# Alternating the three pieces of an expert tile with those of its neighbours in a deformable-convolution and mixture-of-experts kernel

## The chip, the cores and the metric

The kernel runs on one core of one Trainium2 chip. The metric is the device time of one execution in microseconds (us), lower is better. Four executions before the change took 6815.22 to 6824.58 us, with a median of 6822.99 us.

## What is computed

The input `x` is four images of 256 channels and 64x64 pixels in float32. First each pixel is normalised over its channels, and three modulated deformable 3x3 convolutions follow, each with a relu; their result is added to `x`. Then every pixel is a token of 256 numbers, which passes a normalisation and a mixture of eight experts, of which the two with the highest gate weights are used for each token:

```python
def _L0_ffn_ref(x, gate_w, gate_b, W1, b1, W2, b2):
    probs = jax.nn.softmax(xf @ gate_w + gate_b, axis=-1)
    top2_vals, top2_idx = jax.lax.top_k(probs, 2)
    ...
        h = jax.nn.gelu(xf @ w1 + bb1, approximate=False)   # 256 -> 512
        y = h @ w2 + bb2                                    # 512 -> 256
        return (acc + we[:, None] * y, None)
...
x = x + _L0_conv_ref(_ln_c(x), ...)
t = _to_tokens(x)
t = t + _L0_ffn_ref(_ln_t(t), ...)
```

## The kernel before

**Convolution.** Twelve stages (a layer of one image each) run one after the other, the images interleaved. A stage has 8 blocks of 512 pixels, and a block 9 taps, so that there are 864 taps. A tap gathers four tiles from a table in memory (`g`, L496, issued by GpSimd as indirect DMAs), interpolates on VectorE (L502, L507) and ScalarE (L510, into `s`), transposes `s` on TensorE (L525, into a PSUM tile `tp`), copies that on ScalarE (L528, `sT`) and multiplies with the tap's weights (L548, `acc`). The PSUM tag `tp` has three buffers, and every transpose of the kernel uses it.

**Experts.** When the last block of an image is done, its tokens are sorted by expert (`route`, `invert`), and 39 tiles of 256 tokens are made of them; the last image is cut into two groups of 23 tiles, so there are 163 tiles in all. The order of a group's tiles takes one from its first half and one from its second in turn, and each half has its own weight buffer, `w[step % 2]`, of 128 x 2308 numbers. Where a tile has the same expert as the one before it in its half, its load is given row numbers beyond the table (`bounds_check`) and moves nothing.

**One tile, in three pieces.** In `expert`, a generator, the first piece adds the bias to the tile before (`products`: `y`, L884 on VectorE, and its store on SP), transposes the tile's tokens `zt` (L832, into a `tp` tile named `ftp`) and copies them to `zT` (L836 on ScalarE, named `fzT` in the profile; one buffer). The second multiplies with W1: two halves of eight matmul records each into `ph` (L848, one PSUM buffer), each followed by two gelu instructions on ScalarE (L858, `hT`, three buffers). The third multiplies with W2, sixteen matmul records into `py` (L866, one PSUM buffer). The load of the next tile's weights (L792) and tokens (L804, two indirect DMAs into two buffers per tag) stands at the head of the third piece, or at the head of the second while the work is being drained.

**When pieces are put in.** `begin` lays the pieces into the lane `tiles`. After every tap `pump` takes as many as their price allows, a third of the group's pace each: paces are 5 taps a tile for the first two groups, 2 for the third, 1.5 for the fourth and 0 for the last. What is left when the taps are over is drained, three pieces at a time (`drain`, and `settle` between some stages). This is the order in which the program names the instructions. The framework then orders each engine's queue by itself: it takes the earliest named instruction that its own cost model thinks ready, so that instructions of a later piece can come before those of an earlier one. `after(x)` only holds an instruction behind `x` on the same engine; it is used for the indirect DMAs (behind the newest gather) and for `y` (behind the newest L507).

Of the kernel before, what the change touches and what calls it, by code (L numbers as in the profile page):

```python
# [8 lines left out]
F32 = mybir.dt.float32  # L9
I32 = mybir.dt.int32  # L10
AF = mybir.ActivationFunctionType
# [3 lines left out]
P = 128  # L15
H = W = 64
C = 256
CC = C // P
# [13 lines left out]
E = 8  # L32
HID = 512
HC = HID // P
FT_LOG = 8
FT = 1 << FT_LOG
FU = FT // P
# [4 lines left out]
W1N = CC * HID + HC  # L42
W2N = HC * C + C
# [29 lines left out]
class Group:  # L73


    def __init__(self, b, n0, n1):
        self.b, self.n0, self.n1 = b, n0, n1
        self.nm = f"{b}_{n0}"
        self.M = (n1 - n0) * TPB

        self.NF = 2 * self.M * P // FT + E - 1


        self.half = (self.NF + 1) // 2
        self.zt, self.acc, self.gy, self.sums, self.py = {}, [], [], [], None
        self.order = [s // 2 + s % 2 * self.half for s in range(self.NF)]


class Lane:
# [5 lines left out]
    def put(self, taps, fn):  # L95
        self.pieces.append((taps, fn))
# [11 lines left out]
class Weave:  # L108
# [672 lines left out]

    def fetch(self, grp, step):

        if self.w is None:
            self.w = [
                self.wt.tile([P, 2, WINN], F32, tag="wt", name=f"w_{i}").rearrange(
                    "p a b -> p (a b)"
                )
                for i in range(2)
            ]  # L790
        f = grp.order[step]
        self.nc.gpsimd.indirect_dma_start(  # L792
            out=self.w[step % 2][:, : W1N + W2N],
            out_offset=None,
            in_=self.ins["W"],
            in_offset=bass.IndirectOffsetOnAxis(ap=grp.wrow[:, f : f + 1], axis=0),
            bounds_check=E * P - 1,
            oob_is_err=False,
        )
        grp.zt[step] = []  # L800
        for u in range(FU):
            zt = self.ffn.tile([P, C], F32, tag=f"zt{u}", name=f"zt_{grp.nm}_{f}_{u}")
            j = FU * f + u
            self.nc.gpsimd.indirect_dma_start(  # L804
                out=zt,
                out_offset=None,
                in_=grp.zd,
                in_offset=bass.IndirectOffsetOnAxis(ap=grp.tok[:, j : j + 1], axis=0),
            )
            grp.zt[step].append(zt)  # L810

    def fetch_next(self, grp, step):
        if step + 1 < grp.NF:
            with self.after(self.gathered):
                self.fetch(grp, step + 1)

    def expert(self, grp, step):

        nc = self.nc
        if step == 0:  # L820
            self.fetch(grp, 0)
            yield
        self.products(grp)
        f = grp.order[step]
        nm = f"{grp.nm}_{f}"
        w = self.w[step % 2]
        w1, w2 = w[:, :W1N], w[:, W1N : W1N + W2N]
        zt = grp.zt.pop(step)
        tp = self.ps.tile([P, CC, FT], F32, tag="tp", name=f"ftp_{nm}")
        for u in range(FU):  # L830
            for c in range(CC):
                nc.tensor.transpose(  # L832
                    tp[:, c, u * P : (u + 1) * P], zt[u][:, c * P : (c + 1) * P], self.ident
                )
        zT = self.ffn.tile([P, CC, FT], F32, tag="zT", bufs=1, name=f"fzT_{nm}")
        nc.scalar.copy(zT, tp)  # L836
        yield

        beside = not self.draining
        if not beside:  # L840
            self.fetch_next(grp, step)
        hT = []
        for h0 in range(0, HC, 2):
            ph = self.ps1.tile([P, 2, FT], F32, tag="ph", name=f"ph_{nm}_{h0}")
            for h in range(2):
                for c in range(CC):
                    o = c * HID + (h0 + h) * P
                    nc.tensor.matmul(  # L848
                        ph[:, h, :],
                        lhsT=w1[:, o : o + P],  # L850
                        rhs=zT[:, c, :],
                        start=(c == 0),
                        stop=(c == CC - 1),
                    )
            ht = self.ffn.tile([P, 2, FT], F32, tag="hT", bufs=3, name=f"hT_{nm}_{h0}")
            for h in range(2):
                k = CC * HID + h0 + h
                nc.scalar.activation(ht[:, h, :], ph[:, h, :], AF.Gelu, bias=w1[:, k : k + 1])  # L858
            hT.append(ht)
        yield  # L860
        if beside:
            self.fetch_next(grp, step)
        py = self.ps1.tile([P, FU, C], F32, tag="py", name=f"py_{nm}")
        for u in range(FU):
            for h in range(HC):
                nc.tensor.matmul(  # L866
                    py[:, u, :],
                    lhsT=hT[h // 2][:, h % 2, u * P : (u + 1) * P],
                    rhs=w2[:, h * C : (h + 1) * C],
                    start=(h == 0),  # L870
                    stop=(h == HC - 1),
                )
        grp.py = (f, py, w2)

    def products(self, grp):

# [81 lines left out]
        put(3, lambda: self.begin(grp))  # L958

    def begin(self, grp):  # L960
        for step in range(grp.NF):
            gen = self.expert(grp, step)
            for _ in range(3 + (step == 0)):
                self.tiles.put(grp.pace / 3, lambda gen=gen: next(gen, None))
        self.tiles.put(grp.pace / 3, lambda: self.products(grp))
        self.tiles.put(3, lambda: self.end(grp))

    def end(self, grp):
# [159 lines left out]
```

## Time and profile before

| what | value |
|---|---|
| median of four executions | 6822.99 us |
| lowest, highest | 6815.22, 6824.58 us |
| the profiled execution, its span | 6832.07 us, 6829.6 us |
| mean granted TensorE clock | 0.979 |
| matmul records of `acc`, `ph`, `py` | 6912, 2608, 2608 |
| busy: TensorE, VectorE, ScalarE, GpSimd | 91%, 72%, 50%, 65% of the span |
| indirect DMAs: gathers, tokens, weights, combine | 3456, 326, 163, 256 |

In the profile PE is TensorE's matmuls, PEld its weight loads, DVE VectorE, ACT ScalarE, POOL GpSimd and SP the queue that issues plain DMAs; a name followed by q is the engine's own queue. `out<-in` names the tile written and the tiles read, "L848" is a line of the kernel. A line of a waits answer is engine, line, what it waited for, microseconds in total, times, longest. A matmul named once in the code is two records here. The recorded length of a matmul holds its passage through the array, so that the records overlap; the distance between starts is what a matmul costs.

### The profile page before, as it was taken

How to read it: one execution, taken by the hardware profiler on the slowest of the kernel's cores; microseconds unless marked ns; L12 is line 12 of the kernel's file. 1: busy time of each engine (PE TensorE's matmuls, PEld its weight loads, DVE VectorE, ACT ScalarE, POOL GpSimd, SP SyncE). 2: the span in 40 equal slices, each digit the busy share in tenths (PEclk: the TensorE clock that was granted, in tenths of full speed). 3: DMA queues.
4: the chain of work that ended last, by engine and by line, in shares of the span. 5: the costliest groups of instructions: out<-in, count | busy, mean ns of one | idle time of the engine just before them, and what ended most of it. 6: DMA issues, size and time to landing. Idle time of an engine off the chain costs nothing. (4 is left out here: it accounts for less than half of the span.)

```text
span 6829.6 us, 88669 instructions
## 1 busy us (share of the span) xinstructions
PE 6225.5 (91%) x26500; PEld 3518.7 (52%) x26500; DVE 4888.6 (72%) x10829; ACT 3437.7 (50%) x7315; POOL 4423.4 (65%) x4245
## 2 busy tenths in 40 slices
PE   7998888888999999999999999999988899988887
PEld 3443344444445555555555455555555566655665
DVE  6777778778999676667878777667778555687511
ACT  4554555555665444446665454445554444554322
POOL 4555766666667666666667777666666766677543
PEclk9999999999999999999999999999999999999998
DMA  8998999999999999999998999989998888899644
GB/s 287 343 347 315 364 346 377 354 353 380 384 395 356 326 349 341 324 337 343 351 356 315 357 359 363 328 334 329 341 341 306 298 286 274 287 359 331 228 136 123
DMA packets 800315, 2223.69 MB, mean 326 GB/s; under 512 B 104728, under 2 KB 302872, under 8 KB 794080
## 3 DMA queue, kind: packets, MB, share of 16 engines
q0 software_dynamic: 551200, 1947.35, 77.1%
q1 hardware_dynamic: 248640, 270.69, 11.6%
q8 instruction: 215, 3.52, 0.2%
q14 instruction: 260, 2.13, 0.1%
HBM read 2160.68 MB, written 196.40 MB: 345 GB/s over the span
## 5 line engine op out<-in xcount | busy, mean ns | idle before, releaser
L496 POOL DMA_INDIRECT g<-tab,idx x3456 | 3624.1, 1049 | 1844.8 <-DVE s L507 736.7
L548 PE MATMUL acc<-sT,wk 128*128 128x512 f32 x6912 | 3389.9, 603 | 164.5 <-ACT sT L528 150.1
L502 DVE SCALAR_TENSOR_TENSOR g<-g,cf 128x512 f32<-128x512 f32 x3456 | 2560.2, 742 | 409.8 <-DMA g<-tab,idx 406.0
L507 DVE SCALAR_TENSOR_TENSOR s<-g,cf 128x256 f32<-128x256 f32 x3456 | 1660.6, 482 | 714.2 <-PE tp L525 427.5
L528 ACT COPY sT<-tp 128x512 f32<-128x512 f32 x1728 | 1001.1, 586 | 1788.1 <-PE tp L525 1782.6
L510 ACT ACTIVATE s<-s,cf 128x256 f32<-128x256 f32 x3456 | 1645.3, 507 | 418.1 <-DVE s L507 409.3
L548 PEld LDWEIGHTS acc<-sT,wk 128*128 128x128 f32 x6912 | 1160.5, 192 | 965.2 <-issue 644.4
L525 PEld LDWEIGHTS tp<-ident,s 128*128 128x128 f32 x6912 | 875.8, 142 | 1393.9 <-issue 652.4
L525 PE MATMUL tp<-ident,s 128*128 128x128 f32 x6912 | 1261.4, 280 | 209.8 <-ACT s L510 189.8
L848 PE MATMUL ph<-fzT,w 128*128 128x256 f32 x2608 | 689.9, 397 | 65.0 <-ACT fzT L836 34.9
L866 PE MATMUL py<-w,hT 128*128 128x256 f32 x2608 | 656.8, 390 | 43.8 <-ACT hT L858 40.0
L848 PEld LDWEIGHTS ph<-fzT,w 128*128 128x128 f32 x2608 | 484.5, 197 | 198.2 <-ACT fzT L836 61.9
L866 PEld LDWEIGHTS py<-w,hT 128*128 128x128 f32 x2608 | 477.5, 192 | 178.9 <-ACT hT L858 83.1
L858 ACT ACTIVATE hT<-ph,w 128x256 f32<-128x256 f32 x652 | 283.4, 471 | 439.1 <-PE ph L848 418.1
L804 POOL DMA_INDIRECT zt<-z,tok x326 | 333.9, 1024 | 163.9 <-issue 88.3
L351 PE MATMUL po<-win,wo 128*32 128x504 f32 (+1 forms) x2304 | 356.0, 594 | 5.0 <-ACT win L295 3.2
L792 POOL DMA_INDIRECT w<-in_W,wrow x163 | 177.5, 1089 | 269.7 <-issue 104.9
L907 POOL DMA_INDIRECT gy<-ys,slots x256 | 264.1, 1031 | 109.6 <-issue 65.7
L884 DVE TENSOR_TENSOR y<-py,w 128x512 f32<-128x512 f32 x163 | 111.4, 684 | 228.8 <-PE py L866 228.8
L922 DVE SCALAR_TENSOR_TENSOR ta<-gy,cw,ta 128x256 f32<-128x256 f32 x256 | 120.5, 479 | 132.3 <-DMA gy<-ys,slots 77.2
L351 PE MATMUL po<-win_pre,wo 128*32 128x504 f32 (+1 forms) x1152 | 187.0, 610 | 3.4 <-ACT om L360 3.1
L351 PEld LDWEIGHTS po<-win,wo 128*32 128x32 f32 x2304 | 72.8, 109 | 174.4 <-issue 140.5
(152 smaller groups left out, 2980.9 us busy)
## 6 DMA issues: line engine op xcount, KB each, us to landing
tab<-hv SPq DMA_DIRECT2D x512, 128.0 KB
g<-tab,idx POOLq DMA_INDIRECT x3456
ys<-y SPq DMA_DIRECT2D x163, 256.0 KB
tab<-h_pre SPq DMA_DIRECT2D x128, 256.0 KB
wk<-in_conv_w SPq DMA_DIRECT2D x99, 256.0 KB
xc_pre<-in_x SPq DMA_DIRECT2D x32, 512.0 KB
xr_tok<-in_x SPq DMA_DIRECT2D x32, 512.0 KB
t<-t_tok SPq DMA_DIRECT2D x32, 512.0 KB
```

The source lines that it names most:

```text
L351: nc.tensor.matmul(po[g * Q : (g + 1) * Q, :].rearrange("q (r w) -> q r w", w=W)[:, :, x0:x1], lhsT=self.wo[l][:, 3 * ky + kx, c, :], rhs= ...
L496: self.gathered = nc.gpsimd.indirect_dma_start(out=g.rearrange("p x s f -> p (x s f)"), out_offset=None, in_=self.table(*self.stages[i]), ...
L502: nc.vector.scalar_tensor_tensor(g[:, :, 0, :], g[:, :, 1, :], cf[:, j, 0:1], g[:, :, 0, :], ALU.mult, ALU.add,)
L507: self.last = nc.vector.scalar_tensor_tensor(s, g[:, 1, 0, :], cf[:, j, 1:2], g[:, 0, 0, :], ALU.mult, ALU.add)
L510: nc.scalar.activation(s, s, AF.Copy, scale=cf[:, j, 2:3])
L525: self.turned = nc.tensor.transpose(tp[:, c, u * P : (u + 1) * P], ss[u][:, c * P : (c + 1) * P], self.ident)
L528: nc.scalar.copy(self.sT[:, :, t0 * P : (t0 + 2) * P], tp)
L548: nc.tensor.matmul(acc[:, o, :], lhsT=self.wk[k][:, c, o * P : (o + 1) * P], rhs=sT[:, c, :], start=(k == 0 and c == 0), stop=(k == K - 1 ...
L804: self.nc.gpsimd.indirect_dma_start(out=zt, out_offset=None, in_=grp.zd, in_offset=bass.IndirectOffsetOnAxis(ap=grp.tok[:, j : j + 1], axi ...
L848: nc.tensor.matmul(ph[:, h, :], lhsT=w1[:, o : o + P], rhs=zT[:, c, :], start=(c == 0), stop=(c == CC - 1),)
L858: nc.scalar.activation(ht[:, h, :], ph[:, h, :], AF.Gelu, bias=w1[:, k : k + 1])
L866: nc.tensor.matmul(py[:, u, :], lhsT=hT[h // 2][:, h % 2, u * P : (u + 1) * P], rhs=w2[:, h * C : (h + 1) * C], start=(h == 0), stop=(h == ...
```

## The change

The generator `expert` becomes three functions: `tile_turn` (transposes and the copy to `zT`), `tile_hidden` (`products` of the tile before, W1 and gelu) and `tile_out` (W2, then the loads). `begin` lays them in another order: W2 of tile s-1, W1 of tile s, transposes of tile s+1. The loads are split: `tile_out` of tile s issues the weights of tile s+1 and the tokens of tile s+2; while draining, `tile_hidden` of tile s issues the weights of s+1. `have` keeps a load from being issued twice. A group has one piece more. The buffers of all tiles stay as they were.

```diff
-        self.zt, self.acc, self.gy, self.sums, self.py = {}, [], [], [], None
+        self.zt, self.acc, self.gy, self.sums, self.py = [], [], [], [], None
+        self.have = 0
 ...
     def fetch(self, grp, step):
+        if step >= grp.NF:
+            return
+        f = grp.order[step]
+        for u in range(FU):
+            zt = self.ffn.tile([P, C], F32, tag=f"zt{u}", name=f"zt_{grp.nm}_{f}_{u}")
+            j = FU * f + u
+            with self.after(self.gathered):
+                self.nc.gpsimd.indirect_dma_start(out=zt, ...)
+            grp.zt.append(zt)
+
+    def weights(self, grp, step):
+        if step < grp.have or step >= grp.NF:
+            return
+        grp.have = step + 1
 ...
+        with self.after(self.gathered):
             self.nc.gpsimd.indirect_dma_start(
+                out=self.w[step % 2][:, : W1N + W2N],
 ...
+    def tile_turn(self, grp, step):
+        ...
+        tp = self.ps.tile([P, CC, FT], F32, tag="tp", name=f"ftp_{nm}")
+        for u in range(FU):
+            zt = grp.zt.pop(0)
+            ...
+        grp.zT = self.ffn.tile([P, CC, FT], F32, tag="zT", bufs=1, name=f"fzT_{nm}")
+        nc.scalar.copy(grp.zT, tp)
+
+    def tile_hidden(self, grp, step):
+        self.products(grp)
+        if self.draining:
+            self.weights(grp, step + 1)
+        ...  (W1 and gelu as before)
+
+    def tile_out(self, grp, step):
+        if step >= 0:
+            ...  (W2 as before)
+            grp.py = (grp.order[step], py, w2)
+        self.weights(grp, step + 1)
+        self.fetch(grp, step + 2)
 ...
     def begin(self, grp):
+        put, part = self.tiles.put, grp.pace / 3
+        put(part, lambda: (self.weights(grp, 0), self.fetch(grp, 0)))
+        put(part, lambda: self.tile_turn(grp, 0))
         for step in range(grp.NF):
-            gen = self.expert(grp, step)
-            for _ in range(3 + (step == 0)):
-                self.tiles.put(grp.pace / 3, lambda gen=gen: next(gen, None))
-        self.tiles.put(grp.pace / 3, lambda: self.products(grp))
+            put(part, lambda step=step: self.tile_out(grp, step - 1))
+            put(part, lambda step=step: self.tile_hidden(grp, step))
+            put(part, lambda step=step: self.tile_turn(grp, step + 1))
+        put(part, lambda: self.tile_out(grp, grp.NF - 1))
+        put(part, lambda: self.products(grp))
         self.tiles.put(3, lambda: self.end(grp))
```

More of the change, by code (lines that the diff above doesn't have):

```diff
@@ L782, in fetch @@
     def fetch(self, grp, step):
+        if step >= grp.NF:
[5 more added lines that the diff above has]
+            with self.after(self.gathered):
+                self.nc.gpsimd.indirect_dma_start(
+                    out=zt,
+                    out_offset=None,
+                    in_=grp.zd,
+                    in_offset=bass.IndirectOffsetOnAxis(ap=grp.tok[:, j : j + 1], axis=0),
+                )
+            grp.zt.append(zt)
[3 more added lines that the diff above has]
+        grp.have = step + 1
         if self.w is None:
@@ L791, in fetch @@
         f = grp.order[step]
[L792 to L803, printed above, removed]
+        with self.after(self.gathered):
@@ L804, in fetch @@
             self.nc.gpsimd.indirect_dma_start(
-                out=zt,
+                out=self.w[step % 2][:, : W1N + W2N],
                 out_offset=None,
-                in_=grp.zd,
-                in_offset=bass.IndirectOffsetOnAxis(ap=grp.tok[:, j : j + 1], axis=0),
-            )
[L810 to L817, printed above, removed]
-        nc = self.nc
[L820 to L828, printed above, removed]
+                in_=self.ins["W"],
@@ L829, in expert @@
+                in_offset=bass.IndirectOffsetOnAxis(ap=grp.wrow[:, f : f + 1], axis=0),
+                bounds_check=E * P - 1,
+                oob_is_err=False,
+            )
+    def tile_turn(self, grp, step):
+        if step >= grp.NF:
+            return
+        nc = self.nc
+        nm = f"{grp.nm}_{step}"
         tp = self.ps.tile([P, CC, FT], F32, tag="tp", name=f"ftp_{nm}")
         for u in range(FU):
+            zt = grp.zt.pop(0)
             for c in range(CC):
                 nc.tensor.transpose(
-                    tp[:, c, u * P : (u + 1) * P], zt[u][:, c * P : (c + 1) * P], self.ident
+                    tp[:, c, u * P : (u + 1) * P], zt[:, c * P : (c + 1) * P], self.ident
@@ L834, in expert @@
                 )
[L835 to L842, printed above, removed]
+        grp.zT = self.ffn.tile([P, CC, FT], F32, tag="zT", bufs=1, name=f"fzT_{nm}")
+        nc.scalar.copy(grp.zT, tp)
+    def tile_hidden(self, grp, step):
+        nc = self.nc
+        self.products(grp)
+        if self.draining:
+            self.weights(grp, step + 1)
+        w = self.w[step % 2]
+        grp.hT = []
@@ L843, in expert @@
         for h0 in range(0, HC, 2):
-            ph = self.ps1.tile([P, 2, FT], F32, tag="ph", name=f"ph_{nm}_{h0}")
+            nm = f"{grp.nm}_{step}_{h0}"
+            ph = self.ps1.tile([P, 2, FT], F32, tag="ph", name=f"ph_{nm}")
             for h in range(2):
@@ L849, in expert @@
                         ph[:, h, :],
-                        lhsT=w1[:, o : o + P],
-                        rhs=zT[:, c, :],
+                        lhsT=w[:, o : o + P],
+                        rhs=grp.zT[:, c, :],
                         start=(c == 0),
@@ L854, in expert @@
                     )
-            ht = self.ffn.tile([P, 2, FT], F32, tag="hT", bufs=3, name=f"hT_{nm}_{h0}")
+            ht = self.ffn.tile([P, 2, FT], F32, tag="hT", bufs=3, name=f"hT_{nm}")
             for h in range(2):
                 k = CC * HID + h0 + h
[L858 to L873, printed above, removed]
+                nc.scalar.activation(ht[:, h, :], ph[:, h, :], AF.Gelu, bias=w[:, k : k + 1])
+            grp.hT.append(ht)
+    def tile_out(self, grp, step):
+        if step >= 0:
+            w2 = self.w[step % 2][:, W1N : W1N + W2N]
+            py = self.ps1.tile([P, FU, C], F32, tag="py", name=f"py_{grp.nm}_{step}")
+            for u in range(FU):
+                for h in range(HC):
+                    self.nc.tensor.matmul(
+                        py[:, u, :],
+                        lhsT=grp.hT[h // 2][:, h % 2, u * P : (u + 1) * P],
+                        rhs=w2[:, h * C : (h + 1) * C],
+                        start=(h == 0),
+                        stop=(h == HC - 1),
+                    )
+            grp.py = (grp.order[step], py, w2)
+        self.weights(grp, step + 1)
+        self.fetch(grp, step + 2)
     def products(self, grp):
```

## The prediction

> **What bounds the kernel now.** I read the page first: its head, its busy line and its slices.
>
> ```profile
> span 6829.6 us, 88669 instructions
> PE 6225.5 (91%) x26500; PEld 3518.7 (52%) x26500; DVE 4888.6 (72%) x10829; ACT 3437.7 (50%) x7315; POOL 4423.4 (65%) x4245
> PE   7998888888999999999999999999988899988887
> DMA  8998999999999999999998999989998888899644
> ```
>
> From slice 13 on, where expert tiles run beside taps, TensorE and the DMA engines are both at eight or nine tenths; only in the last three slices does the DMA fall off. The kernel is shared between two limits until about 6330 us and is a chain of expert tiles after that. I therefore split the waits there. First the stretch with both (2160 to 6330 us), in the view of waits; the last two numbers of a line are how often and the longest.
>
> ```profile
> PE tp L525 <- ACT s L510: 115.3, 132, 2.8
> PE acc L548 <- ACT sT L528: 40.6, 68, 1.6
> PE ph L848 <- ACT fzT L836: 34.9, 51, 1.3
> PE py L866 <- ACT hT L858: 24.1, 48, 1.4
> PE ph L848 <- ACT hT L858: 4.8, 7, 1.8
> PE tp L525 <- ACT sT L528: 4.1, 4, 1.4
> ...
> DVE g L502 <- DMA g<-tab,idx: 373.1, 249, 10.8
> DVE s L507 <- PE tp L525: 303.4, 308, 4.7
> ```
>
> Within the tiles' three steps TensorE waits 34.9 + 24.1 + 4.8 = 63.8 us here; these are what the change can touch. The last two lines say who is behind whom in the taps: VectorE waited 303 us for TensorE to free `s`, and 373 us for gathers to land. So TensorE is the limit in about 303 / (303 + 373) = 45% of it.
>
> Then one tile of that stretch in the timeline (start, duration, engine; in brackets the idle time before and who ended it):
>
> ```profile
> 4326.15 0.60 PE L832 MATMUL ftp<-ident,zt 128*128 128x128 f32 x4
> 4327.43 0.70 PE L848 MATMUL ph<-fzT,w 128*128 128x256 f32 x2 [0.67 <-ACT fzT L836]
> ...
> 4334.38 0.70 PE L866 MATMUL py<-w,hT 128*128 128x256 f32 x2 [0.35 <-ACT hT L858]
> ```
>
> The transposes and the W1 products are named a whole piece apart (5/3 taps), yet run next to each other: the framework pulls a piece forward once its inputs should be there. So the waits come from adjacency in that order, not in the program's. Last, the drain:
>
> ```profile
> 6727.59 1.89 PE L848 MATMUL ph<-fzT,w 128*128 128x256 f32 x8
> ...
> 6729.31 0.60 PE L832 MATMUL ftp<-ident,zt 128*128 128x128 f32 x4
> ...
> 6730.58 1.89 PE L848 MATMUL ph<-fzT,w 128*128 128x256 f32 x8
> ...
> 6733.09 2.86 PE L866 MATMUL py<-w,hT 128*128 128x256 f32 x12 [0.19 <-ACT hT L858]
> ```
>
> Between the two halves of W1 stand the transposes of a later tile: the framework has already moved them ahead of this tile's W2. W2 begins every 8.20 us here (6733.09, 6741.29, 6749.49). TensorE's waits from 6330 to 6780 us:
>
> ```profile
> PE ph L848 <- DMA w<-in_W,wrow: 24.5, 9, 8.6
> PE py L866 <- ACT hT L858: 15.9, 21, 8.0
> ```
>
> **The change part by part.**
>
> *Transposes moved ahead of W2.* Per tile they issue four records at L832, no DMA, and one copy (0.586 us). In the stretch before 6330 us, `ph` of tile s+1 now finds `zT` filled, since sixteen W2 records (3.45 us in the chain of waits) and the copy lie between. That removes the 51 waits, 34.9 us. Bounds: 0 if the framework still sets them side by side, 34.9 if all go. I take 34.9. What is late next there is `w`, taken up below.
>
> *Transposes as filler.* The tokens of tile s+2 are asked for a tile earlier, so the four transposes (0.6 us a set) can stand in a gelu wait. 55 waits cost 24.1 + 4.8 = 28.9 us, 0.53 us each; a set fits one of a tile's two gaps, and some are filled by taps already. Bounds 0 to 28.9; I take 12, somewhat under half.
>
> *The drain.* About 40 tiles (644 `ph` weight loads from 6330 us on, 16 each). Work per tile by starts: 32 records of 0.217 us (eight take 1.74) plus 0.57 us of transposes is 7.5 us of the 8.20, so 0.7 us is lost, 28 us in all. But the transposes of the next tile are already pulled between the halves, and the rest is gelu, whose distance to its users does not change. I take 0; bounds 0 to 28 gained.
>
> *Weights one piece later against their use.* Each group issues the same loads in the same order; `w` of s+1 still stands two pieces behind `y` of s-1, which frees its buffer, so GpSimd's queue waits for the same thing as now, and behind it stand the token loads and the next gathers. But its use comes one piece later instead of two. In the trace a load at 5501.79 us was used at 5520.80, 19 us on, at pace 2, where a piece is two thirds of a tap of 10 us. Losing a piece leaves 12.3 us. Landing took 7.46 and 8.64 us in the drain (chain), where the DMA is half idle. No row shows it beside busy gathers; 8.64 us scaled by the DMA shares of the two stretches (0.93 to 0.50 in the view by windows) is an estimate of 16 us, so 0 to 3.7 us for each load that moves data. The drain waited on 9 loads in its last 29 tiles, so I count 9 in a group, and two groups have a short pace: 0 to 67 us. At pace 5 (load at 4328.16, use at 4364.97, 37 us) a piece is 12 us and 25 us is left: nothing. I take 0 in all, nearest to the 12.3 us against 8.64. In the drain `w` waits for `y` as before: 0.
>
> The Trainium skill speaks against this part. Its page "DMA: Bandwidth & Descriptors", section "Rules for kernel authors", asks for a DMA to be issued early and waited on late; the section "Bandwidth" gives 6.15 us for 1 MB, an estimate of 7.3 us for this tile's 1.18 MB. This trace's 7.46 and 8.64 us agree in size. By the page's figure a load under 12.3 us of cover costs nothing and the sum stays 47 us; by its rule alone, each late load counts and the sum is reduced.
>
> *Token loads two pieces ahead instead of one.* TensorE waited for them 0.5 us before 6330 us and 1.1 us after: worth 0 to 2, I take 0. In the drain GpSimd's queue is in order, and the token loads no longer stand right behind a blocked `w`; they were not waited for, so 0.
>
> *The copy to `zT`.* It now waits also for the second half of W1 of the tile before, because `zT` has one buffer. Queued behind it on ScalarE are the scalings of `s` (L510) and the copies of `sT` (L528), for which TensorE's taps wait. Rival B prices it; in the sum 0, since ScalarE is 50% busy.
>
> *`products`, the extra piece.* `y` and its store on SP stay four pieces behind their tile's load; one more piece per group issues nothing: 0. The first load of a group is now held behind a gather, five times about 1 us of GpSimd that nobody waits for: 0.
>
> Sum: 34.9 + 12 = 47 us of TensorE waits. Where gathers are the limit, TensorE would only wait for `s` instead, so I keep 45%: 21 us. Against the profiled execution that is 6832 - 21 = 6811 us; it stood 9 us above the median of 6822.99, so the median goes to 6802 us. A measurement of this kernel can tell about 0.2%, 14 us, from no change.
>
> **The rivals.**
>
> *A: no change.* The waits move to the next one on TensorE, `s`, which already costs 115.3 us, because gathers set the pace, or the framework's order hardly moves, as in the drain. For it: the DMA at nine tenths, 343 GB/s; against: the 303 us by which VectorE waited on TensorE. 6823, 6810 to 6836. Chance 0.17.
>
> *B: slower, by the shared `tp` buffers.* Transposes of tile s+1 can run as soon as their tokens land, before tile s has its W1 products, and hold one of three `tp` buffers until ScalarE's copy, which waits for those products. Today the hold is 1.2 us (4326.15 to 4327.38); W1 of one tile spreads over 13.5 us in the same timeline (4327.43 to 4340.90), and the hold could be that long. The taps want a buffer every 3.6 us (24 taps in slice 16's 171 us, two pairs each). Waits for a buffer are 4.1 us today, so nothing shows how two buffers do; the price is one copy and its signal, 0.75 us, for each of 123 tiles outside the drain: 92 us, at 45% 42, less the 21 won: 6844 us, and up to 6894 without the factor. It decides once more than half a wait per tile comes of it. Chance 0.24.
>
> *C: slower, by weights.* If loads land later than 12.3 us, up to 67 us less the 21: up to 6869. Chance 0.06.
>
> *D: more.* All 63.8 us go and TensorE is the limit throughout: 6759. With the drain's 28, 6731. Chance 0.10.
>
> **How the numbers follow.** The forecast (6790 to 6809) has 0.43, A 0.17, B 0.24, C 0.06, D 0.10. Faster is the forecast and D, 0.53; within 0.2% is A, 0.17; slower is B and C, 0.30. The range goes from just under D's first figure to a third of the way up B's: 6758 to 6862. Left out are D's second figure and the upper parts of B and C, nearly 0.2. The forecast's own range is 6790 to 6809.
>
> **What would show it.** Right: TensorE's wait of `ph` for `fzT` falls from 34.9 us to a few, `py` for `hT` to about half, `ph` for `w` stays nil before 6330 us, VectorE's wait for `tp` falls, and the drain's step stays 8.2 us. Wrong: waits of `tp` for `sT` rise from 4.1 us to tens (B); `ph` waits for `w` before 6330 us (C); the wait of L525 for `s` grows by what `fzT` lost (A); the drain's step falls towards 7.5 us (D).

## The result, and the profile after

Forty executions after the change have a median of 6834.68 us, sixty before it on the same chip 6824.32 us: a ratio of 1.0015, with a 95% interval of 1.0010 to 1.0019. The change makes the kernel slower by about 10 us, where the prediction said 21 us faster. The profiled execution took 6840.62 us. Of the experiments below, some ran on chips where the kernel before itself took 7,643 to 7,762 us; each ratio is against the kernel before on the same chip, these runs are marked "slow chip", and neither the change itself nor the kernel with late tokens (experiment 6) was timed on such a chip.

The page's busy line hardly moves:

```profile
PE 6224.5 (91%) x26500; PEld 3504.5 (51%) x26500; DVE 4897.4 (72%) x10829; ACT 3441.7 (50%) x7309; POOL 4414.1 (65%) x4245
```

TensorE does the same work in the same busy time. The view of waits from 2160 to 6330 us, TensorE's lines, after the change (engine, line, what it waited for; us in total, times, longest):

```profile
PE tp L526 <- ACT s L511: 143.6, 173, 3.1
PE acc L549 <- ACT sT L529: 91.5, 144, 1.8
...
PE tp L526 <- ACT sT L529: 5.1, 4, 4.0
PE py L876 <- ACT hT L866: 3.5, 2, 2.8
...
PE ph L856 <- ACT hT L866: 1.9, 5, 0.4
...
PE ph L856 <- ACT fzT L840: 0.7, 1, 0.7
...
PE ph L856 <- DMA w<-in_W,wrow: 0.5, 1, 0.5
```

The three waits that the change could touch fell from 34.9 + 24.1 + 4.8 = 63.8 us to 0.7 + 3.5 + 1.9 = 6.1 us. But the taps' two grew: `tp` for `s` from 115.3 to 143.6 us, `acc` for `sT` from 40.6 to 91.5 us, 79.2 us together. All waits of TensorE in this window rose from 282 to 298 us: it now waits more, not less. VectorE, in the same window and view:

```profile
DVE g L503 <- DMA g<-tab,idx: 365.4, 272, 10.2
DVE s L508 <- PE tp L526: 298.3, 228, 7.3
```

These were 373.1 and 303.4 us: who is behind whom in the taps has not changed. One tile in the timeline shows why `acc` waits:

```profile
2717.46 0.44 PE L526 MATMUL tp<-ident,s 128*128 128x128 f32 x2
2718.58 1.12 PE L549 MATMUL acc<-sT,wk 128*128 128x512 f32 x2 [0.67 <-ACT sT L529]
2719.54 1.89 PE L856 MATMUL ph<-fzT,w 128*128 128x256 f32 x8
2721.26 1.88 PE L549 MATMUL acc<-sT,wk 128*128 128x512 f32 x4
```

The eight records of half of W1 stand in one block, and the tap's products stand right behind its transposes, so they wait for the copy to `sT`. Before, the framework had cut W1 into pieces that stood between a tap's transposes and its products, which then waited for nothing:

```profile
2730.67 0.64 PE L525 MATMUL tp<-ident,s 128*128 128x128 f32 x2
2731.09 1.91 PE L848 MATMUL ph<-fzT,w 128*128 128x256 f32 x4
2732.80 1.20 PE L548 MATMUL acc<-sT,wk 128*128 128x512 f32 x2
```

Over the whole trace, W1's 2608 records (`ph`) lie in 515 runs of 5.1 on TensorE before and in 339 runs of 7.7 after, and a run of `ph` follows directly on `tp` 229 times before and 36 times after. W1 was the filler for the taps; with its waits gone from one place it no longer fills another. This alone does not set the time: the kernel of experiment 2 has 511 such runs and is as slow as the change, that of experiment 6 has 341 and is the fastest.

In the drain (timeline):

```profile
6735.44 2.86 PE L876 MATMUL py<-w,hT 128*128 128x256 f32 x12 [0.19 <-ACT hT L866]
...
6743.64 2.86 PE L876 MATMUL py<-w,hT 128*128 128x256 f32 x12 [0.19 <-ACT hT L866]
```

The step is 8.20 us, as before.

**Where the time goes by stage.** The ends of the twelve stages, counted from 0, are read from the timeline as the last relu of each stage's last block (L570 before, L571 after). Stages 0 to 3 take the same time in all kernels of this table within 1 us each. The others, and the tail from there to the end of the span, in us of one profiled execution each (the last three columns are experiments told below, on chips where the kernel before took its usual time):

| stage | before | after | null | old order, new loads | tokens late |
|---|---|---|---|---|---|
| 4 to 6 | 1553 | 1551 | 1557 | 1556 | 1555 |
| 7 | 541 | 555 | 535 | 545 | 550 |
| 8 | 521 | 527 | 523 | 524 | 527 |
| 9 | 518 | 533 | 517 | 514 | 526 |
| 10 | 654 | 635 | 648 | 656 | 606 |
| 11 | 636 | 643 | 636 | 641 | 631 |
| tail | 423 | 411 | 414 | 419 | 406 |

So the change loses 14 us in stage 7, 21 us in stages 8 and 9 and 7 us in stage 11, and wins 19 us in stage 10 and 12 us in the tail. (The rows are rounded; the spans differ by 9.3 us.)

*Stage 7* loses in a single block, the third, which takes 26 us more (14 us come back in the next one). There a group ends and its combine begins. GpSimd's longest wait in it, in the timeline of after, with the store's owner on VectorE:

```profile
3714.14 6.10 PE L876 MATMUL py<-w,hT 128*128 128x256 f32 x16 [0.33 <-DVE tok L781]
3720.28 0.69 DVE L897 TENSOR_TENSOR y<-py,w 128x512 f32<-128x512 f32 x1 [4.21 <-PE py L876]
3721.00 0.37 SPq L900 DMA_DIRECT2D ys<-y  x1
3723.99 0.95 POOL L920 DMA_INDIRECT gy<-ys,slots  x1 [13.76 <-DMA ys<-y]
```

The combine's first load `gy` waits 13.76 us for the store of the group's last `y`, whose W2 now runs just ahead of it, and the gathers queue behind. Before, no line of GpSimd's waits in that block (3668 to 3732 us) comes to more than 2.7 us in all. The block takes 89 to 90 us in the two kernels of the table with the new order of pieces and 64 to 67 us in the three with the old one.

*Stage 9* has no such event: VectorE waits 4.5 us for gathers in all there before and not at all after, so the taps' chain through TensorE is likely what is long. TensorE's lines of waits in that stage, before (4599 to 5117 us) and after (4617 to 5150 us):

```profile
PE tp L525 <- ACT s L510: 16.7, 18, 1.2
PE ph L848 <- ACT fzT L836: 8.1, 12, 0.7
PE acc L548 <- ACT sT L528: 6.8, 10, 0.7
PE py L866 <- ACT hT L858: 6.5, 9, 1.4
```

```profile
PE tp L526 <- ACT s L511: 34.0, 36, 1.9
PE acc L549 <- ACT sT L529: 18.9, 29, 1.0
```

These are all its lines after; before there are three small ones more, 3.0 us together. So 41.1 us became 52.9 us, 11.8 us more, where the stage takes 15 us more. (With tokens late it is 45.4 us, 4.3 more than before, and the stage takes 8 us more.) The waits are most of the loss, not all of it.

### The profile page after: what moved, and what is told of

It is laid out like the page before. It is cut to its first block, busy times and chain, and to the rows that moved or that the text cites. A ratio compares the mean times of both kernels' runs of the same rounds, so it can differ in the third digit from the quotient of the medians.

```text
span 6838.9 us, 88616 instructions
## 1 busy us (share of the span) xinstructions
PE 6224.5 (91%) x26500; PEld 3504.5 (51%) x26500; DVE 4897.4 (72%) x10829; ACT 3441.7 (50%) x7309; POOL 4414.1 (65%) x4245
## 5 line engine op out<-in xcount | busy, mean ns | idle before, releaser
L508 DVE SCALAR_TENSOR_TENSOR s<-g,cf 128x256 f32<-128x256 f32 x3456 | 1661.7, 482 | 717.6 <-PE tp L526 421.9
L526 PE MATMUL tp<-ident,s 128*128 128x128 f32 x6912 | 1282.2, 281 | 231.8 <-ACT s L511 218.3
L856 PE MATMUL ph<-fzT,w 128*128 128x256 f32 x2608 | 633.4, 385 | 20.1 <-DMA w<-in_W,wrow 17.3
```

The costliest lines, as they stand in the source:

```text
L508: self.last = nc.vector.scalar_tensor_tensor(s, g[:, 1, 0, :], cf[:, j, 1:2], g[:, 0, 0, :], ALU.mult, ALU.add)
L526: self.turned = nc.tensor.transpose(tp[:, c, u * P : (u + 1) * P], ss[u][:, c * P : (c + 1) * P], self.ident)
L856: nc.tensor.matmul(ph[:, h, :], lhsT=w[:, o : o + P], rhs=grp.zT[:, c, :], start=(c == 0), stop=(c == CC - 1),)
```

## The experiments

**1. The null.** One empty piece more per group in the kernel before; it deals the framework's order anew and does nothing else.

```diff
         self.tiles.put(grp.pace / 3, lambda: self.products(grp))
+        self.tiles.put(grp.pace / 3, lambda: None)
```

> The kernel before, with one empty piece more at the end of each group: no work is added or moved, but the later groups' pieces come a third of a tile later and the framework orders some queues anew. If a change of 0.15% is more than the chance of a new order, this stays within 5 us of the kernel before; if new orders alone move the time by that much, it is off by 8 to 20 us in either direction.

Measured on a slow chip: 1.0008 (0.9991 to 1.0025). Repeated:

> The kernel before with one empty piece more per group: nothing is computed, loaded or waited for more, only the framework's order is dealt anew. If a new order alone moves the time by the size of the change's +0.15%, this differs from before by 0.05 to 0.2% in either direction, and the +0.15% carries no cause of its own. If it stays within 0.05%, the change's loss has a cause that can be found.

6817.72 against 6825.04 us: 0.9991 (0.9982 to 1.0000). A new deal of the same work moves the time by about 0.1%, here in stages 7 and 10 and in the tail. The change's 0.15% is not much more than that, so small differences of one stage are not to be given a cause each.

**2. The old order with the new loads.** The change's split loads and early tokens, with the pieces of a tile laid as before.

```diff
+        put(part, lambda: (self.weights(grp, 0), self.fetch(grp, 0), self.fetch(grp, 1)))
...
-            put(part, lambda step=step: self.tile_out(grp, step - 1))
+            put(part, lambda step=step: (self.products(grp), self.tile_turn(grp, step)))
             put(part, lambda step=step: self.tile_hidden(grp, step))
-            put(part, lambda step=step: self.tile_turn(grp, step + 1))
...
+            put(part, lambda step=step: self.tile_out(grp, step))
```

> The changed kernel with its pieces in the old order (transposes, W1, W2 of one tile), but with the tokens asked for a tile earlier as in the change. If the order of the pieces is what moved the waits, TensorE's wait of W1 for the copied tokens is back at 30 to 40 us, that of the taps' products for sT at 40 to 50 us, and the time is that of the kernel before within 7 us. If the early tokens matter, the waits look like the changed kernel's (under 5 us, and about 90) and it is 10 us slower than before.

Slow chip: 0.9987 (0.9965 to 1.0008). Repeated:

> The changed kernel with its pieces in the old order and the early tokens of the change, once more, because in its first comparison even the kernel before took 7759 us, with waits for nothing that the profile shows of up to 4 us each on every engine. Where the kernel before takes about 6824 us: if the order of the pieces moved the waits, W1's wait for the copied tokens is 30 to 40 us, the products' wait for sT 40 to 50 us, and the time that of the kernel before within 7 us. If the early tokens matter: the waits of the changed kernel (under 5 and about 90 us), and 10 us slower than before.

6829.69 against 6818.95 us: 1.0014 (1.0005 to 1.0023), as slow as the change, though its view of waits (2160 to 6330 us) is much that of the kernel before. Of the two answers expected, the waits are the first and the time is the second:

```profile
PE tp L526 <- ACT s L511: 126.0, 148, 3.1
PE acc L549 <- ACT sT L529: 40.2, 67, 1.6
PE ph L856 <- ACT fzT L840: 29.5, 45, 0.7
PE py L876 <- ACT hT L866: 26.5, 48, 2.8
```

So it made no difference between these two that some 55 us of TensorE's waits stood at the tiles in the one and at the taps in the other, and the loss may as well lie with the loads.

**3. Gelus held back.** If ScalarE's queue were the place (a gelu that waits for W1 holds up the scalings and copies behind it), the gelus' place in it should matter. In both orders each gelu was held behind the newest scaling of `s`.

```diff
+            self.scaled = nc.scalar.activation(s, s, AF.Copy, scale=cf[:, j, 2:3])
...
+                with self.after(self.scaled):
                     nc.scalar.activation(ht[:, h, :], ph[:, h, :], AF.Gelu, ...)
```

> The changed kernel, with every gelu held behind the newest scaling of s on ScalarE. Theory S: the gelus stand too early in ScalarE's in-order queue, wait there for W1 (379 us against 172 us before) and hold up scalings and copies; then this wait falls below 250 us, the products' wait for sT falls from 91 us towards 50, and the time falls by 10 to 30 us. Theory F (W1 no longer fills the gap between a pair's transposes and the products): the gelus' place does not matter, the products still wait about 90 us, time within 8 us of the changed kernel. Theory G (gathers set the pace): time within 8 us too.

> The kernel before with the same hold on its gelus. Theory S: ScalarE's wait of gelu for W1 falls from 172 us, and the time by up to 10 us. Theories F and G: no change beyond that of a new order, within 10 us.

Slow chip: 1.0055 (1.0037 to 1.0073) in the change's order, 1.0061 (1.0037 to 1.0086) in the old one. Both lose the same against the kernel before, so this does not tell the two orders apart, and ScalarE's order is not shown to be where the change lost.

**4. Half of W2 left out.** Of four matmuls over the hidden units two are done, 8 records of 0.217 us, 1.73 us a tile.

```diff
-                for h in range(HC):
+                for h in range(2):
...
-                        stop=(h == HC - 1),
+                        stop=(h == 1),
```

> The changed kernel with half of the W2 products left out (8 of 16 records per tile, 1.73 us of TensorE). If TensorE is the limit beside the experts, the 123 tiles before the drain save up to 213 us and the 40 drained ones up to 69: 200 to 280 us in all. If gathers are (theory G), only the drain saves: 50 to 90 us in all.

> The kernel before with half of the W2 products left out: the same two answers, 200 to 280 us if TensorE is the limit, 50 to 90 us if gathers are.

Slow chip: 1.0164 (1.0136 to 1.0191) with the change and 0.9995 (0.9974 to 1.0016) without it; 282 us less of TensorE's work gave nothing there. Repeated with the change:

> The changed kernel with half of the W2 products left out (1.73 us of TensorE per tile), once more for the same reason. TensorE the limit beside the experts: 200 to 280 us saved in all. Gathers the limit (theory G): only the drain saves, 50 to 90 us in all.

6772.88 against 6818.95 us: 0.9931 (0.9916 to 0.9947). The same kernel lost 1.6% on a slow chip and wins 0.7% here, so what only a slow chip shows is not carried over. Against the span after the change it saves 69 us: 51 in the tail (360 us) and 18 up to the end of stage 11, where some 123 of the 163 tiles left out 123 x 1.73 = 213 us. Beside the taps the kernel kept 18 / 213 = 8% of what was taken from TensorE, and perhaps less, since the ratios put the whole saving at 57 us and not 69. Much of the rest came back as waits of TensorE for the taps' inputs (2160 to 6330 us):

```profile
PE tp L526 <- ACT s L511: 198.4, 269, 2.7
PE acc L549 <- ACT sT L529: 152.6, 236, 2.0
```

143.6 + 91.5 = 235.1 us rose to 351.0 us, and all its waits there from 298 to 428 us. TensorE is busy for 93% of the time there (2459 of 2632 us from 2485 to 5117 us, after the change), and yet less work for it hardly shortens the stages. The kernel before had this cut on a slow chip only.

**5. Half of every gather left out.** The gathers load the first half of a row's 4 KB, and the interpolation takes one pixel of that half for all four.

```diff
-                out=g.rearrange("p x s f -> p (x s f)"),
+                out=g[:, 0].rearrange("p s f -> p (s f)"),
...
-                g[:, :, 0, :], g[:, :, 1, :], cf[:, j, 0:1], g[:, :, 0, :],
+                g[:, :, 0, :], g[:, 0:1, 1, :].to_broadcast([P, 2, C]), cf[:, j, 0:1],
+                g[:, 0:1, 1, :].to_broadcast([P, 2, C]),
```

> The changed kernel with half the bytes of every gather of the taps (one of two neighbouring columns is left out, VectorE's two instructions keep their sizes). Theory G: gathers set the pace beside the experts, so the time falls by several per cent and, with TensorE now alone at the limit, this kernel is faster than the kernel before with the same cut by 20 to 50 us. Theory F: TensorE is the limit already beside the experts, the time falls mostly in the stages without experts (by up to 250 us), and the two cut kernels are within 12 us of each other.

> The kernel before with half the bytes of every gather. Theory G: 20 to 50 us slower than the changed kernel with that cut. Theory F: within 12 us of it.

Slow chip: 1.0043 (1.0028 to 1.0059) and 1.0132 (1.0093 to 1.0170). Repeated on a chip where the kernel before took 6825.04 us:

> The change with only the first half of every gather's bytes loaded (the second row's values are taken from the first half, so the output is another one). If the gathers' transfers set the pace beside the experts, the block period there falls from 64.5 us towards the 57 us of the blocks without experts: 40 blocks times up to 7 us, so up to 280 us less, 0.96 to 0.985 of before, and VectorE's 365 us of waits for gathers mostly go. If a loop through VectorE, ScalarE and TensorE sets it, 0.995 or more, and the waits of VectorE for tp grow by what those for gathers lose.

> The same in the kernel before (half of every gather left out). The pair tells whether the change's order is worth something once transfers are short: if TensorE then is the limit beside the experts, the change with half gathers is 20 to 60 us (0.3 to 0.9%) faster than this kernel; if not, the two are within 0.2%.

7541.37 and 7548.05 us: 1.1050 (1.1032 to 1.1068) and 1.1059 (1.1043 to 1.1076). No theory said this. VectorE waits longer for gathers (2160 to 6330 us, in the old order; 373.1 us with whole gathers), and GpSimd longer for VectorE's `s`, which frees a gather's buffer (416.6 us with whole ones):

```profile
DVE g L502 <- DMA g<-tab,idx: 1398.2, 1222, 7.6
...
POOL g L496 <- DVE s L508: 904.4, 576, 9.4
```

But a gather is not slower. Taking the n-th gather of GpSimd with the n-th L502, from the end of its issue to VectorE's start it took a median of 2.7 us where VectorE had waited for it, and 5.4 us with whole gathers. What changed is VectorE's order. Before, the two steps of the interpolation alternate (L507 stands in 3366 runs for 3456 instructions). Now the framework has put several first steps ahead of as many second ones (1080 runs, most often of four). The queues, POOL being GpSimd's:

```profile
3004.20 3.25 DVE L508 SCALAR_TENSOR_TENSOR s<-g,cf 128x256 f32<-128x256 f32 x8
3008.20 0.96 POOL L496 DMA_INDIRECT g<-tab,idx  x1 [0.31 <-issue]
...
3011.81 0.75 DVE L502 SCALAR_TENSOR_TENSOR g<-g,cf 128x512 f32<-128x512 f32 x1 [0.84 <-DMA g<-tab,idx]
...
3019.33 1.67 DVE L508 SCALAR_TENSOR_TENSOR s<-g,cf 128x256 f32<-128x256 f32 x4
```

Since the second step frees the buffer, buffers come free late and in groups, and a gather is issued a median of 2 gathers ahead of its use, where it was 8. So this is no test of the bytes' price: the cut also dealt VectorE a worse order, and the trace lays the loss there, without a run that parts the two.

**6. Tokens asked for late again.** The change's order, with one edit: the token rows of tile s+1 are asked for in the piece of W1 of tile s, one piece ahead of their transposes, instead of two.

```diff
     def tile_hidden(self, grp, step):
...
+        self.fetch(grp, step + 1)
         w = self.w[step % 2]
...
     def tile_out(self, grp, step):
...
         self.weights(grp, step + 1)
-        self.fetch(grp, step + 2)
```

> The change's order of pieces, with the token rows asked for one piece ahead as in the kernel before. If the early token loads are what costs (they were in the old-order kernel that lost 0.14% too), this is back at 1.000 of before or better, down to 0.997 if the order of pieces is a gain that they hid. If the order or a new deal of it costs, it stays near 1.0015.

6773.14 against 6825.04 us: 0.9924 (0.9910 to 0.9937), a version faster than both kernels, by 52 us against before and some 61 us against the change, more than either answer expected and far beyond the null's 0.09%. Its profile differs from the change's in the stages at the end, by 29 us in stage 10, 12 in stage 11 and 7 in stage 9. Stage 10 is that of the group with pace 2, and GpSimd's queue there goes round in a loop. The timeline of the change:

```profile
5414.68 1.15 POOL L814 DMA_INDIRECT w<-in_W,wrow  x1 [2.26 <-ACT fzT L840]
5416.13 1.10 POOL L792 DMA_INDIRECT zt<-z,tok  x1 [0.30 <-issue]
5417.54 0.97 POOL L792 DMA_INDIRECT zt<-z,tok  x1 [0.30 <-issue]
5418.82 0.97 POOL L920 DMA_INDIRECT gy<-ys,slots  x1 [0.30 <-issue]
5420.09 0.95 POOL L920 DMA_INDIRECT gy<-ys,slots  x1 [0.30 <-issue]
5421.35 0.95 POOL L497 DMA_INDIRECT g<-tab,idx  x1 [0.30 <-issue]
...
5434.88 1.15 POOL L814 DMA_INDIRECT w<-in_W,wrow  x1 [3.69 <-ACT win L296]
```

and VectorE's in the same stretch:

```profile
5413.20 0.69 DVE L897 TENSOR_TENSOR y<-py,w 128x512 f32<-128x512 f32 x1
...
5433.41 0.68 DVE L897 TENSOR_TENSOR y<-py,w 128x512 f32<-128x512 f32 x1
```

The profile puts the wait of `w` down to ScalarE, but every weight load from 5395 to 5773 us is issued 0.78 or 0.79 us after a `y` ends, so it is `y`, the last reader of the weights' buffer, that it waits for. Behind it stand two token loads, two combine loads and then eight gathers; after them comes the next `w`. This step takes 19.9 us (19 steps from 5395.28 to 5773.22 us), and was 20.0 us before (20 steps from 5365.34 to 5765.47 us), where the same row stands:

```profile
5423.75 1.15 POOL L792 DMA_INDIRECT w<-in_W,wrow  x1 [2.24 <-ACT s L510]
5425.20 1.10 POOL L804 DMA_INDIRECT zt<-z,tok  x1 [0.30 <-issue]
...
5444.64 1.15 POOL L792 DMA_INDIRECT w<-in_W,wrow  x1 [3.89 <-ACT hv L322]
```

With tokens late:

```profile
5414.19 1.21 POOL L792 DMA_INDIRECT zt<-z,tok  x1 [0.30 <-issue]
5415.71 0.96 POOL L792 DMA_INDIRECT zt<-z,tok  x1 [0.30 <-issue]
...
5422.44 1.01 POOL L814 DMA_INDIRECT w<-in_W,wrow  x1 [0.30 <-issue]
5423.75 0.96 POOL L920 DMA_INDIRECT gy<-ys,slots  x1 [0.30 <-issue]
```

Four gathers stand between the token loads and the weight load. The step is 18.1 us (19 steps from 5387.54 to 5731.98 us), and GpSimd's waits at the weight load in stage 10 fall from 62 to 27 us (67 before). Nineteen steps at 1.8 us are 34 us, about what the stage won. In that stage VectorE's waits for gathers fall from 162.5 us in the change to 118.3 us, and ScalarE's for VectorE's L508 from 158.7 to 56.0 us.

**7. Is it the row of loads, or their being early?** Late tokens also stand apart from the weights. Three kernels try to part the two. First, the old order with tokens a piece ahead of the weights, so that the same four gathers stand between them:

```diff
-    def fetch_next(self, grp, step):
+    def fetch_next(self, grp, step, load):
...
-                self.fetch(grp, step + 1)
+                load(grp, step + 1)
...
-        if not beside:
-            self.fetch_next(grp, step)
+        self.fetch_next(grp, step, self.rows if beside else self.fetch)
...
         if beside:
-            self.fetch_next(grp, step)
+            self.fetch_next(grp, step, self.weights)
```

> The order of pieces of the kernel before, with a tile's token rows asked for one piece ahead of its weights, so that on GpSimd four gathers stand between the two instead of none. Theory Q (GpSimd's queue: a weight load that waits there for y holds the token loads, the combine's loads and then the gathers): most of what the kernel with late tokens won comes here too, 0.992 to 0.996, the stage of 654 us (the fourth from the end) falls to 605 to 625 us, and GpSimd's waits at the weight load there fall from 62 us towards 16. Theory O (the new order of pieces is what wins, once tokens are late): 0.999 to 1.002 and that stage stays near 650 us.

Slow chip: 1.0045 (1.0024 to 1.0067). Run once more, again on a slow chip:

> The order of pieces of the kernel before with token rows and weights four gathers apart on GpSimd, on a chip where the kernel before takes its usual time. If the row of loads behind the waiting weight load is all, this takes most of what the kernel with late tokens won: 0.992 to 0.996, the fourth stage from the end at 605 to 625 us (654 before, 606 with late tokens), GpSimd's waits at the weight load there near 27 us. If the new order of pieces is needed too, as the disturbed run hinted (waits at the weight load did not fall there), 0.999 to 1.005, that stage at 645 us or more and its waits at 60 us or more.

1.0039 (1.0021 to 1.0057). Loads that stand apart do not win by themselves there: stage 10 takes 793 us, against 738 us of the null on another slow chip, GpSimd's waits at the weight load are 168 us against 126 us, and nearly every weight load still comes 0.79 us after a `y`. So the row alone is not shown to be the cause; what this kernel does where the kernel before takes its usual time was not seen.

Second, the change with tokens as early as they were and the weights asked for in the piece of W1, right behind `y`:

```diff
     def tile_hidden(self, grp, step):
...
-        if self.draining:
-            self.weights(grp, step + 1)
+        self.weights(grp, step + 1)
...
     def tile_out(self, grp, step):
...
-        self.weights(grp, step + 1)
         self.fetch(grp, step + 2)
```

> The change's order and its early token loads (two pieces ahead), with the weights asked for in the piece of W1, so that gathers stand between a weight load and the token rows. Theory Q: 0.991 to 0.996, like the kernel with late tokens, since it is the row of loads behind a waiting weight load that costs; though the weights now stand right behind y, GpSimd may wait longer at them, up to 60 us as in the change. Theory T (a token load that is early costs as such, by its buffer or by its transfer beside the gathers): stays at 1.000 to 1.003.

Slow chip: 1.0885 (1.0847 to 1.0922), 8444.13 us. GpSimd's view of waits over the whole span says why:

```profile
POOL w L814 <- DVE g L503: 428.7, 33, 26.4
POOL w L814 <- ACT s L511: 269.8, 33, 19.7
```

Weight loads wait up to 26 us, and all gathers behind them. It doesn't answer the question that it was made for, since it moved the weights as well; it does show, on that chip, what a blocked queue can cost.

Third, the change with tokens earlier still, in the piece of the transposes:

```diff
     def tile_turn(self, grp, step):
...
+        self.fetch(grp, step + 1)
         grp.zT = self.ffn.tile([P, CC, FT], F32, tag="zT", bufs=1, ...)
...
         self.weights(grp, step + 1)
-        self.fetch(grp, step + 2)
```

> The change with the token rows asked for three pieces ahead, in the piece of the transposes: where the pace is short, they then stand right in front of the weight load instead of right behind it, and the combine's loads still follow, so GpSimd's row of five stays; where the pace is long they stand apart. Theory Q: little is won where the pace is short (that stage stays at 625 to 640 us), 0.997 to 1.001 in all. Theory T: slower than the change, 1.002 or more, as the tokens are earlier still.

Slow chip: 1.0144 (1.0119 to 1.0170), on the side of the theory of early tokens; against the null on another slow chip, 98 of its 110 us lie in stages 5 to 9, where the pace is long, and none in stage 10 (734 against 738 us). But the change was not timed on a slow chip, so the 1.0144 may hold the new order's own cost there, and the old order with early tokens lost nothing on one (experiment 2). What is shown is experiment 6: the place of the token loads on GpSimd's queue decides 0.9% of this kernel in the change's order, and with late tokens stage 10 has a shorter step. Whether the row or the earliness does it stays open.

## Why the prediction was wrong

*"Token loads two pieces ahead": "worth 0 to 2, I take 0": the step that decides the sign.* The prediction priced these loads by what TensorE waited for them, and not by what stands with them on GpSimd's queue, though it named the token loads and gathers that stand behind a waiting weight load. Put back by one piece, with nothing else changed, they take the kernel from 1.0015 to 0.9924 of before, some 61 us, three times the 21 us of the forecast. In stage 10 the loop through that queue set the step before the change and after it, and late tokens shorten the step by 1.8 us. In the old order early tokens cost only 0.14% (experiment 2), so it is the two together that cost, and why is open.

*"TensorE is the limit in about 45%", and so 21 us kept: the step that failed in the sum itself.* The ratio of VectorE's two waits was read as a share of time in which TensorE's idle time counts. Experiment 4 measured what the kernel keeps: 8% of the work left out beside the taps. And the sum held only the waits that go. Nothing in it asked what the W1 records had been covering: between a tap's transposes and its products they hid the copy to `sT`. When they moved, 50.9 us came up there and 28.3 us at `s`, 79 us against 58 us that went. Where the taps are likely the chain, in stage 9, the net of the waits is 12 of the 15 us lost. The kernel with late tokens is no late proof of the forecast: its waits moved like the change's (`acc` for `sT` 94.6 us, from 2160 to 6330 us), in stages 7 to 9 it is 23 us slower than before, and it wins in stages 10 and 11 and the tail.

*Rival A: nearest.* The measured 6834.68 us lies in its 6810 to 6836, and its sign came: the wait for `s` grew by 28.3 us where `fzT` lost 34.2. It said nothing of the loads. `acc` for `sT`, second in the view of before with 40.6 us, came up only beside the copy to `zT`, where it was put at 0 because ScalarE is 50% busy.

*Transposes ahead of W2: right for the wait.* 34.9 us of waits for `fzT` became 0.7 us, as taken.

*Transposes as filler: more than said.* 28.9 us became 5.4 us, 23.5 gone where 12 were taken.

*Weights one piece later: "I take 0": right.* Their cover held (`ph` for `w` 0.5 us before 6330 us), so rival C was wrong in its mechanism. The Trainium skill's page "DMA: Bandwidth & Descriptors", section "Rules for kernel authors", asks for a DMA to be issued early; the runs show a limit of that rule, since token loads asked for a piece earlier cost 61 us in this order.

*The end of a group: not in the sum.* The prediction looked at the extra piece ("issues nothing: 0"), and the null has it too without a loss. But in the new order a group's last W2 runs right ahead of the combine, and GpSimd stood 13.8 us for the last store (13.5 us with tokens late). Stage 7 lost 14 us with the change and 9 us with tokens late, and its third block is long in the kernels of the new order alone.

*The drain: right.* The step stayed 8.20 us. The tail's 12 us are no sign: the null's tail is 9 us shorter as well.

*Rival B: wrong.* Waits of `tp` for `sT` went from 4.1 to 5.1 us.

What remains of the 10 us: the change's order with late tokens wins 0.76%, the early tokens take that and more. Since the null moves 0.09%, no finer account of the 0.15% is claimed.

## What to carry to other kernels

Before counting a removed wait as time, ask what the moved instructions were covering where they stood, and test by leaving work out whether that engine's time is kept at all: here 213 us less of a 93% busy engine gave 18. When you leave work out, look whether the queues kept their order, or you measure the new order instead (experiment 5). Price a load that moves by its place on its queue, and not only by who waits for it. On a queue that issues DMAs in order, follow a blocked load to the loads behind it and round the loop to what unblocks it (`y`, weights, tokens, combine, gathers, `y`); the length of that loop was the step of a stage, and the profile's name for the releaser was not the real one. Run a null that only deals the order anew, so that you know which differences are worth a cause.

## What the hardware showed that was not expected

With half the bytes, and fewer gathers in flight, a gather was there 2.7 us after its issue instead of 5.4 us, where VectorE waited for it, and yet the kernel took 10.5% longer, with gathers issued only 2 ahead of their use instead of 8. On three chips the kernel before took 7,643 to 7,762 us, 12 to 14% longer; in the null's trace on such a chip TensorE's transposes of the taps wait 140 us for "issue" from 2460 to 7200 us, in 60 waits of up to 16.8 us, where the profile of before shows one wait for issue of 1.9 us on all of TensorE. Its cause is not known.
